# Layer 0's softmax sums and layer 1's transposes by VectorE and transfers, layer 1's moves issued by GpSimd

## The chip, the cores and the metric

The kernel runs on one core of a Trainium2 chip. The metric is the device time of one execution in microseconds (us): a median of 3161.45 us over three runs (3160.39 to 3161.61). A profile records one further execution, engine by engine: PE is TensorE (PEld its weight loads), DVE is VectorE, ACT is ScalarE, POOL is GpSimd, and SPq is the queue in which SyncE issues transfers. PSUM is the memory that TensorE writes; TensorE, VectorE and ScalarE each take their instructions in order.

## What is computed

The input x is (4, 128, 64, 64) in float32: four batches, 128 channels, 4096 tokens each. Two layers follow each other, cut here to what matters:

```python
# layer 0, on _gn(x): q, k, v and gate are 1x1 convolutions with scale and bias
attn = jax.nn.softmax(jnp.einsum('bdn,bdm->bnm', q, k), axis=-1)
out = jnp.einsum('bcm,bnm->bcn', v.reshape(B, -1, N), attn)
x = x + _conv_bn(out.reshape(B, -1, H, W) * gate, Wp, sp, bp)
# layer 1, on tokens t (4, 4096, 128)
q = jnp.einsum('bsd,de->bse', _ln_t(t), W)
t = t + softmax(q @ q.T) @ _ln_t(t)
Wx = batch_norm(_ln_t(t) @ W_ffn.T)        # then a recurrent scan over the tokens
t = t + scan(lambda y, wx: sigmoid(wx + y @ V.T))
```

Both softmaxes need a row sum for each token (the "denominator"), by which the weighted values are divided.

## The kernel before

Each batch is worked through in two stages. The 4096 tokens are cut into 8 blocks of 512 (`NB`, `QB`), and each block into 4 tiles of 128 (`NQ`). Layer 0 (`attention`, lines 178 to 220) takes block n after block n, and for each block 16 pairs of key tiles. Each pair gives two score products (line 200), one exponential on ScalarE (line 202, into one of four buffers `e`), an addition into `acc` on VectorE (lines 207 and 209), and, two pairs later (`LAG`), four weighted products (line 383). Layer 1 (`layer1`, lines 435 to 600) uses that its scores are symmetric: for a pair of blocks (n, a) it computes scores once (line 562), exponentials (line 568), a product with the values (`direct`, line 455), and a second product with the transposed exponentials (`reversed_products`, line 468). The transposed exponentials come from a VectorE transpose of 32x32 squares (line 573) into `dd` and 16 transfers from `dd` to `tt` (line 594), all issued by SyncE. The rows of blocks run in the order 6, 7, 5, 4, 3, 2, 1, 0.

When a block is complete, `finish` appends small closures to the list `pending`; the loops call one of them at each step. Work for the next batch stands in a second list, `ahead`. In layer 0 a block's closures are these:

- `sums`: `denominators` (lines 222 to 233) adds the two halves of `acc` on VectorE (line 224), multiplies each of the 4 tiles by a column of ones on TensorE (line 227, result `md`), and copies and inverts the result (lines 232 and 233). Then `move` turns the residual `xb` into tokens.
- `projection`: one product (line 409) and a `move` of the result into `yt`.
- `tokens`: multiply and add (line 414), layernorm (`layernorm`, lines 250 to 263, whose inverse square root is two GpSimd instructions, lines 116 and 117), and a `move` of the normalised tokens into `ht`.
- `queries`: one product (line 424) on `ht`.

A `move` (lines 235 to 246) transposes 128 x 512 values: a VectorE transpose of 32x32 squares into a buffer `d` (two buffers, line 241), one transfer to a DRAM tile `turn_d` (line 244), and four transfers back (line 246), which wait for the first. All five are issued by SyncE.

In layer 1 a block's closures are `tokens` (row sums at lines 507 and 508, four TensorE transposes of `oacc` into `mt` at line 511, multiply and add at line 513, layernorm), `result` (four TensorE transposes into `mr` at line 523, a ScalarE copy at line 525 and one transfer to `t2_d` at line 526), `turn` (four TensorE transposes of `h2` into `mh` at line 531, a ScalarE copy into `th` at line 532) and `inputs` (one product `mw` on `th` at line 536, statistics and a copy on VectorE at lines 537 and 543, and a transfer at line 544).

The order in which instructions stand on each engine is made at build time by a scheduler from the program and its dependencies; semaphores are put in where one engine needs another's result.

## Time and profile before

| | us |
|---|---|
| median of three runs | 3161.45 |
| the profiled execution | 3160.82 |
| its span, first to last instruction | 3159.1 |
| TensorE busy | 3069.4 |
| VectorE busy | 1797.1 |
| ScalarE busy | 1125.2 |
| GpSimd busy | 140.6 |
| sum products `md`, line 227, 256 records | 33.3 |
| transposes `mt`, line 511, 128 records | 20.0 |
| transposes `mr`, line 523, 128 records | 19.6 |
| transposes `mh`, line 531, 128 records | 28.3 |

Records of one engine overlap, since matmuls are pipelined: what a group occupies is better read from the starts of the instructions around it than from the sum of its records. Each product of 512 columns in float32 shows as two records. Layer 0 of the second batch lies at 820 to 1164 us of the span, its layer 1 at 1164 to 1570; batches three and four follow in the same rhythm, and the recurrent scan is the last 86 us.

### The profile page before, as it was taken

Reading aid. Unit: us, or ns where it says so; the run is one execution under the profiler, and the core shown is the slowest. Engines: PE = TensorE matmul, PEld = TensorE weight load, DVE = VectorE, ACT = ScalarE, POOL = GpSimd, SP = SyncE. Lnnn points to the kernel's source line nnn. Section 1 sums busy time; section 2 is a strip of 40 time slices with the busy share of each in tenths; the row PEclk is TensorE's granted clock in tenths of the full one; section 3 lists DMA queues with packets and bytes.
Section 4 is the critical chain, followed back from the end, with each engine's and each line's share of the span. In section 5 each row is a group of like instructions: output and inputs, shape, how many; then the busy total and the mean of one; then the engine's idle time right before and its main releaser. Section 6 shows DMA issues by size and latency. Waiting matters only on the chain.

```text
span 3159.1 us, 32271 instructions
## 1 busy us (share of the span) xinstructions
PE 3069.4 (97%) x10762; PEld 1374.7 (44%) x10762; DVE 1797.1 (57%) x2970; ACT 1125.2 (36%) x1978; POOL 140.6 (4%) x183
## 2 busy tenths in 40 slices
PE   7999999999999999999999999999999999999976
PEld 3444444444444444444444444444444444444433
DVE  6555556555555555555555555555555555455556
ACT  3433333333333333333333333333333333222324
POOL 0000000000000000000000000000000000000000
PEclk9999999999999999999999999999999999999988
DMA  1111133333111123333211113333321112543333
GB/s 50 34 47 54 54 95 93 91 91 92 51 50 54 54 64 94 94 92 93 74 51 54 54 37 102 92 94 92 91 55 54 54 41 66 146 102 90 99 117 156
DMA packets 233934, 242.17 MB, mean 77 GB/s; under 512 B 88736, under 2 KB 144544, under 8 KB 232736
## 3 DMA queue, kind: packets, MB, share of 16 engines
q1 hardware_dynamic: 233760, 240.02, 27.5%
q8 instruction: 88, 1.44, 0.2%
q14 instruction: 86, 0.70, 0.1%
HBM read 65.80 MB, written 56.62 MB: 39 GB/s over the span
## 4 chain that ended last, share of the span: by engine, by line
PE 89%; DVE 5%; SPq 2%; POOL 1%; DMA 1%; issue 1%; ACT 0%; DVEq 0%; ACTq 0%; POOLq 0%
PE o L383 28%; PE ps L200 15%; PE o L455 13%; PE ps L562 13%; PE ot L468 11%; SPq L594 2%; PE mt L409 1%; PE mw L536 1%; PE mq L424 1%; PE md L227 1%; PE pg L350 1%; PE pqk L315 1%; PE pv L335 1%; PE mh L531 1%; POOL rstd L117 1%
## 5 line engine op out<-in xcount | busy, mean ns | idle before, releaser
L383 PE MATMUL o<-e,nxt 64*128 64x512 f32 x4096 | 965.4, 589 | 0.0
L202 ACT ACTIVATE e<-ps 128x1024 f32<-128x1024 f32 x512 | 521.2, 1024 | 740.6 <-PE ps L200 734.4
L209 DVE TENSOR_TENSOR acc<-acc,e 128x1024 f32<-128x1024 f32 x448 | 546.4, 1220 | 386.7 <-ACT e L202 375.3
L568 ACT ACTIVATE e<-ps,shift 128x512 f32<-128x512 f32 x576 | 391.2, 684 | 772.8 <-PE ps L562 483.2
L383 PEld LDWEIGHTS o<-e,nxt 64*128 64x128 f32 x4096 | 399.5, 187 | 482.7 <-issue 474.6
L562 PE MATMUL ps<-qt 128*128 128x512 f32 x1152 | 546.7, 595 | 3.0 <-ACT e L568 3.0
L200 PE MATMUL ps<-nxt 64*128 64x512 f32 x2048 | 537.9, 603 | 0.3 <-ACT e L202 0.3
L455 PE MATMUL o<-e,h 128*128 128x512 f32 x1152 | 533.4, 592 | 0.0
L468 PE MATMUL ot<-tt,h 128*128 128x512 f32 x896 | 406.6, 597 | 3.6 <-DMA tt<-dd 3.5
L573 DVE STREAM_TRANSPOSE dd<-e 128x512 f32<-128x512 f32 x448 | 288.7, 685 | 109.0 <-ACT e L568 61.3
L455 PEld LDWEIGHTS o<-e,h 128*128 128x128 f32 x1152 | 216.9, 190 | 260.2 <-issue 259.0
L562 PEld LDWEIGHTS ps<-qt 128*128 128x128 f32 x1152 | 211.8, 191 | 243.2 <-issue 222.7
L200 PEld LDWEIGHTS ps<-nxt 64*128 64x128 f32 x2048 | 188.8, 187 | 245.4 <-issue 161.2
L468 PEld LDWEIGHTS ot<-tt,h 128*128 128x128 f32 x896 | 170.2, 191 | 218.2 <-issue 214.1
L473 DVE TENSOR_REDUCE slots<-tt 128x4 f32<-128x2048 f32 x112 | 252.8, 2258 | 8.6 <-DMA tt<-dd 8.2
L482 DVE TENSOR_TENSOR oacc<-oacc,ot 128x512 f32<-128x512 f32 x88 | 59.9, 681 | 209.2 <-PE ot L468 209.2
L116 POOL TENSOR_SCALAR rstd<-mv 128x4 f32<-128x4 f32 x64 | 14.5, 227 | 2518.9 <-DVE mv L257 2518.9
L568 ACT ACTIVATION_READ_ACCUMULATOR e<-ps,shift 128x1 f32 x576 | 113.1, 196 | 0.0
L401 POOL TENSOR_SCALAR xb<-xb,bpc 128x512 f32<-128x512 f32 x32 | 53.6, 1676 | 323.9 <-DMA xb<-in_x_dram 301.5
L117 POOL TENSOR_TENSOR rstd<-rstd,mhalf 128x4 f32<-128x4 f32 x64 | 66.4, 1037 | 5.3
L700 PE MATMUL ps_r<-y,w 128*128 128x256 f32 x168 | 53.0, 440 | 9.7 <-ACT y L697 6.2
L260 DVE TENSOR_SCALAR h<-t,mv,rstd 128x128 f32<-128x128 f32 x128 | 35.7, 343 | 45.2 <-POOL rstd L117 45.2
(113 smaller groups left out, 1411.8 us busy)
## 6 DMA issues: line engine op xcount, KB each, us to landing
tt<-dd SPq DMA_DIRECT2D x1792, 64.0 KB, 2.0
turn_d<-d SPq DMA_DIRECT2D x96, 256.0 KB, 2.0
t_d<-t SPq DMA_DIRECT2D x64, 256.0 KB, 2.0
nxt<-in_x_dram SPq DMA_DIRECT2D x16, 512.0 KB, 6.4
xb<-in_x_dram SPq DMA_DIRECT2D x32, 256.0 KB, 2.9
t<-turn_d SPq DMA_DIRECT2D x128, 64.0 KB, 2.0
yt<-turn_d SPq DMA_DIRECT2D x128, 64.0 KB, 2.0
ht<-turn_d SPq DMA_DIRECT2D x128, 64.0 KB, 2.0
```

The source lines that it names most:

```text
L117: nc.gpsimd.tensor_tensor(dst, dst, mhalf[:, :n], ALU.pow)
L200: nc.tensor.matmul(ps[:, h, :], lhsT=lhsT, rhs=rhs, start=True, stop=True)
L202: nc.scalar.activation(e, ps, AF.Exp, scale=scale)
L209: nc.vector.tensor_tensor(acc, acc, e, ALU.add)
L383: nc.tensor.matmul(o[r], lhsT=v[rs, p + h * PAIRS, :], rhs=e[rs, h, :], start=(p == 0 and h == 0), stop=(p == PAIRS - 1 and h == 1),)
L455: nc.tensor.matmul(o, lhsT=h[:, NQ * a + 2 * i + half, :], rhs=e[:, half, :], start=(a == n and i == 0 and half == 0), stop=(a == 0 and i ...
L468: nc.tensor.matmul(ot, lhsT=h[:, NQ * n + j, :], rhs=t[:, :, j, :, :].rearrange("q p k j -> q k p j"), start=(j == 0), stop=(j == NQ - 1),)
L473: nc.vector.tensor_reduce(slots[:, bass.ts(n, NQ), a], t.rearrange("q p b k j -> q b p (k j)"), AX.XY, ALU.add,)
L562: nc.tensor.matmul(ps[:, half, :], lhsT=qt[:, bass.ts(at, P)], rhs=qt[:, bass.ts(n, QB)], start=True, stop=True,)
L568: nc.scalar.activation(e[:, half, :], ps[:, half, :], AF.Exp, bias=shift, accum_out=slots[:, at, n : n + 1],)
L573: nc.vector.transpose(d.rearrange("q f b k j -> q k b f j")[:, 2 * i + half], e[:, half, :].rearrange("q (b f j) -> q b f j", b=NQ, f=NQ),)
L594: nc.sync.dma_start(t[bass.ts(f, 32), p], d[bass.ts(p, 32), f])
```

## The change

- Layer 0: `denominators` no longer uses TensorE. After the addition of the halves, VectorE transposes 32x32 squares of `acc` into `dq`, reduces 128 x 512 to 128 x 16, and five transfers (one to a DRAM tile `den_d`, four back into `rq`) bring the partial sums to their tokens. A small reduction in `tokens` completes them.
- Layer 1: for all but the last batch's blocks 0 and 1 (`late`), the transposes of `oacc` and of `h2` become `move`s whose transfers are issued by GpSimd (`nc.gpsimd`), `turn` falls away, and the closure `tokens` is cut in two (`weighted`, `tokens`) with empty closures between. For all blocks, `result` becomes a VectorE transpose and four transfers by SyncE, in place of four TensorE transposes, a ScalarE copy and one transfer.
- Work from `ahead` is now also taken along with closures that hold no TensorE work (`light`). The two `acc` buffers become one tile. After the first block of each layer 0, whatever is left in `pending` is called at once (`flush`).

```diff
-                        acc = accp.tile([P, 2, QB], F32, tag="acc", name="acc", bufs=2)
+                        acc = accs[:, n % 2]
...
+                    if n == 0 and p == PAIRS - 1:
+                        flush()
...
-        def denominators(acc, at, rinv):
+        def denominators(acc, at):
             nc.vector.tensor_tensor(acc[:, 0, :], acc[:, 0, :], acc[:, 1, :], ALU.add)
-            m = ps_m.tile([P, NQ], F32, tag="m", name="md")
-            for j in range(NQ):
-                nc.tensor.matmul(
-                    m[:, j : j + 1], lhsT=acc[:, 0, bass.ts(j, P)], rhs=ones,
-                    start=True, stop=True,
-                )
-            den = den_all[:, at : at + NQ]
-            nc.vector.tensor_copy(den, m)
-            nc.vector.reciprocal(rinv, den)
-
-        def move(blocks, dst):
+            d = work.tile([P, 16, 32], F32, tag="d", name="dq", bufs=2)
+            nc.vector.transpose(d, acc[:, 0, :].rearrange("p (b k) -> p b k", k=32))
+            r = stat.tile([P, 16], F32, tag="r", name="r", bufs=2)
+            nc.vector.tensor_reduce(r, d, AX.X, ALU.add)
+            via = den_d[n_moves % len(den_d)]
+            rq = stat.tile([P, 4, NQ], F32, tag="rq", name="rq", bufs=2)
+            nc.sync.dma_start(via, r)
+            for f in range(4):
+                nc.sync.dma_start(
+                    rq[bass.ts(f, 32)],
+                    via[:, bass.ts(f, NQ)].rearrange("(p k) j -> k p j", p=4),
+                )
+            return rq
+
+        def move(blocks, dst, queue=nc.sync):
...
-            nc.sync.dma_start(via, d)
+            queue.dma_start(via, d)
             for a in range(4):
-                nc.sync.dma_start(dst[bass.ts(a, 32)], via[:, a].rearrange("(p i) j k -> i p j k", p=4))
+                queue.dma_start(dst[bass.ts(a, 32)], via[:, a].rearrange("(p i) j k -> i p j k", p=4))
...
                 def tokens():
+                    den = den_all[:, at : at + NQ]
+                    nc.vector.tensor_reduce(den, parts[0].rearrange("q p j -> q j p"), AX.X, ALU.add)
+                    nc.vector.reciprocal(rinv, den)
...
+                late = b == B - 1 and n < 2
+                def weighted():
                     at = (B + b) * NT + n * NQ
                     den = den_all[:, at : at + NQ]
                     nc.vector.tensor_reduce(den, slots[:, bass.ts(n, NQ), :], AX.X, ALU.add)
                     nc.vector.reciprocal(rinv, den)
-                    m = ps_m.tile([P, NQ, P], F32, tag="m", name="mt")
-                    for j in range(NQ):
-                        nc.tensor.transpose(m[:, j, :], oacc[:, n, bass.ts(j, P)], ident)
+                    if not late:
+                        move(oacc[:, n, :].rearrange("c (j f k) -> c j f k", j=NQ, f=4), ot, nc.gpsimd)
+                def tokens():
...
-                    layernorm(quarters(t1), quarters(h2))
+                    layernorm(tiles(t), quarters(h2))
+                    if not late:
+                        move(
+                            h2.rearrange("q j (p i) -> q j p i", p=4),
+                            th.rearrange("c (f j k) -> c f j k", f=4, j=NQ), nc.gpsimd,
+                        )
                 def result():
-                    m = ps_m.tile([P, QB], F32, tag="m", name="mr")
-                    for j in range(NQ):
-                        nc.tensor.transpose(m[:, bass.ts(j, P)], t1[:, j, :], ident)
-                    t2 = work.tile([P, QB], F32, tag="xb", name="t2")
-                    nc.scalar.copy(t2, m)
-                    nc.sync.dma_start(t2_d[b, :, cs], t2)
+                    d = work.tile([P, 4, NQ, 32], F32, tag="d", name="d", bufs=2)
+                    nc.vector.transpose(
+                        d.rearrange("q p j k -> q j p k"), t.rearrange("q p j i -> q j p i")
+                    )
+                    to = t2_d[b, :, cs].rearrange("(p i) (f r) -> f i p r", p=4, f=4)
+                    for f in range(4):
+                        nc.sync.dma_start(
+                            to[f], d[bass.ts(f, 32)].rearrange("i p j k -> i p (j k)")
+                        )
...
-                pending.extend([tokens, result, turn, inputs])
+                if late:
+                    pending.extend([weighted, tokens, turn, inputs, result])
+                else:
+                    light.update([weighted, tokens, result])
+                    pending.extend([weighted, nothing, tokens, result, nothing, inputs])
...
-                        if pending:
-                            pending.popleft()()
-                        elif ahead:
+                        item = pending.popleft() if pending else nothing
+                        item()
+                        if item in light and ahead:
                             ahead.popleft()()
```

More of the change, by code (lines that the diff above doesn't have):

```diff
@@ L66, in conv_attn_hybrid_kernel @@
     t_d = dram.tile([B, NB, P, 4, NQ, 32], F32, name="t_d")
+    den_d = [dram.tile([P, 16], F32, name=f"den{i}_d") for i in range(4)]
     turn_d = [dram.tile([P, 4, NQ, 32], F32, name=f"turn{i}_d") for i in range(8)]
@@ L120, in conv_attn_hybrid_kernel @@
     fast(
-        tc, x, out, t_d, t2_d, wxs_d, turn_d,
+        tc, x, out, t_d, t2_d, wxs_d, turn_d, den_d,
         dict(qk=w[:, DQ : DQ + P], vs=w_vs, g=w_g, ps=w_ps, a=w_a, f=w_f, vt=v_t),
@@ L143, in fast @@
 def fast(
-    tc, x, out, t_d, t2_d, wxs_d, turn_d, wt, col, par, par2, bpc, bc, ident, gavg, ones,
+    tc, x, out, t_d, t2_d, wxs_d, turn_d, den_d, wt, col, par, par2, bpc, bc, ident, gavg, ones,
     shift, inv_sqrt, par_ok,
@@ L171, in fast @@
         done = set()
+        light = {nothing}
         def flush(until=None):
@@ L182, in attention @@
             o = None
+            accs = accp.tile([P, 2, 2, QB], F32, tag="acc", name="acc")
             def pop():
@@ L218, in attention @@
                         pending.popleft()()
+                    if n == 0 and p == PAIRS - 1:
+                        flush()
             while fifo:
                 pop()
-        def denominators(acc, at, rinv):
+        def denominators(acc, at):
+            nonlocal n_moves
             nc.vector.tensor_tensor(acc[:, 0, :], acc[:, 0, :], acc[:, 1, :], ALU.add)
-            m = ps_m.tile([P, NQ], F32, tag="m", name="md")
-            for j in range(NQ):
-                nc.tensor.matmul(
-                    m[:, j : j + 1], lhsT=acc[:, 0, bass.ts(j, P)], rhs=ones,
-                    start=True, stop=True,
-                )
-            den = den_all[:, at : at + NQ]
-            nc.vector.tensor_copy(den, m)
-            nc.vector.reciprocal(rinv, den)
-        def move(blocks, dst):
+            d = work.tile([P, 16, 32], F32, tag="d", name="dq", bufs=2)
[9 more added lines that the diff above has]
+                    via[:, bass.ts(f, NQ)].rearrange("(p k) j -> k p j", p=4),
+                )
+            return rq
+        def move(blocks, dst, queue=nc.sync):
             nonlocal n_moves
@@ L267, in tiles, with by_tile @@
             return [t[:, :, j, :] for j in range(NQ)]
+        def by_tile(t):
+            return t.rearrange("c (f j k) -> c j f k", f=4, j=NQ)
         def quarters(t):
@@ L401, in finish @@
                 nc.gpsimd.tensor_scalar(xb, xb, bpc, None, ALU.add)
+                at = b * NT + n * NQ
+                parts = []
                 def sums():
-                    denominators(acc, b * NT + n * NQ, rinv)
-                    move(xb.rearrange("c (j f k) -> c j f k", j=NQ, f=4), t)
+                    parts.append(denominators(acc, at))
+                    move(by_tile(xb), t)
                 def projection():
@@ L409, in projection @@
                     nc.tensor.matmul(m, lhsT=wt["ps"], rhs=og, start=True, stop=True)
-                    move(m.rearrange("c (j f k) -> c j f k", j=NQ, f=4), yt)
+                    move(by_tile(m), yt)
                 def tokens():
+                    den = den_all[:, at : at + NQ]
+                    nc.vector.tensor_reduce(den, parts[0].rearrange("q p j -> q j p"), AX.X, ALU.add)
+                    nc.vector.reciprocal(rinv, den)
                     for j in range(NQ):
@@ L498, in finish @@
                 t = work.tile([P, 4, NQ, 32], F32, tag="t", name="t1", bufs=2)
+                ot = work.tile([P, 4, NQ, 32], F32, tag="og", name="otk")
                 h2 = work.tile([P, NQ, C], F32, tag="h2", name="h2")
                 th = work.tile([P, QB], F32, tag="th", name="th")
-                t1 = work.tile([P, NQ, C], F32, tag="og", name="t1b")
                 nc.sync.dma_start(t, t_d[b, n])
-                def tokens():
+                late = b == B - 1 and n < 2
+                def weighted():
                     at = (B + b) * NT + n * NQ
@@ L508, in tokens @@
                     nc.vector.reciprocal(rinv, den)
-                    m = ps_m.tile([P, NQ, P], F32, tag="m", name="mt")
-                    for j in range(NQ):
-                        nc.tensor.transpose(m[:, j, :], oacc[:, n, bass.ts(j, P)], ident)
+                    if not late:
+                        move(oacc[:, n, :].rearrange("c (j f k) -> c j f k", j=NQ, f=4), ot, nc.gpsimd)
+                def tokens():
+                    src = ot
+                    if late:
+                        m = ps_m.tile([P, NQ, P], F32, tag="m", name="mt")
+                        for j in range(NQ):
+                            nc.tensor.transpose(m[:, j, :], oacc[:, n, bass.ts(j, P)], ident)
+                        src = m.rearrange("q j (p i) -> q p j i", p=4)
@@ L512, in tokens @@
                     for j in range(NQ):
                         nc.vector.scalar_tensor_tensor(
-                            t1[:, j, :].rearrange("q (p i) -> q p i", p=4),
-                            m[:, j, :].rearrange("q (p i) -> q p i", p=4), rinv[:, j : j + 1],
-                            t[:, :, j, :], ALU.mult, ALU.add,
-                        )
-                    layernorm(quarters(t1), quarters(h2))
-                def result():
-                    m = ps_m.tile([P, QB], F32, tag="m", name="mr")
-                    for j in range(NQ):
-                        nc.tensor.transpose(m[:, bass.ts(j, P)], t1[:, j, :], ident)
-                    t2 = work.tile([P, QB], F32, tag="xb", name="t2")
-                    nc.scalar.copy(t2, m)
-                    nc.sync.dma_start(t2_d[b, :, cs], t2)
+                            t[:, :, j, :], src[:, :, j, :], rinv[:, j : j + 1], t[:, :, j, :],
@@ new lines, in tokens @@
+                            ALU.mult, ALU.add,
+                        )
+                    layernorm(tiles(t), quarters(h2))
[4 more added lines that the diff above has]
+                        )
+                def result():
+                    d = work.tile([P, 4, NQ, 32], F32, tag="d", name="d", bufs=2)
[7 more added lines that the diff above has]
+                        )
@@ L530, in turn @@
                     for j in range(NQ):
-                        nc.tensor.transpose(m[:, bass.ts(j, P)], h2[:, j, :], ident)
+                        nc.tensor.transpose(by_tile(m)[:, j], h2[:, j, :], ident)
                     nc.scalar.copy(th, m)
@@ L544, in inputs @@
                         nc.sync.dma_start(wxs_d[b, :, :, bass.ts(n, GB), :], wx)
-                pending.extend([tokens, result, turn, inputs])
+                if late:
+                    pending.extend([weighted, tokens, turn, inputs, result])
+                else:
+                    light.update([weighted, tokens, result])
+                    pending.extend([weighted, nothing, tokens, result, nothing, inputs])
             for n in [NB - 2, NB - 1] + list(range(NB - 3, -1, -1)):
```

## The prediction

> **What bounds the kernel now.** I read the busy shares first, then the busy time by stage (the second batch's layer 0 and layer 1), then the chain of waits.

> ```profile
> PE 3069.4 (97%) x10762; PEld 1374.7 (44%) x10762; DVE 1797.1 (57%) x2970; ACT 1125.2 (36%) x1978; POOL 140.6 (4%) x183
> ```

> ```profile
> 820.00:1164.00 344.00, 344.00 (x1562) 152.06 (x1562) 199.37 (x304) 133.19 (x138) 23.63 (x24) 1.00 0.16 49
> 1164.00:1570.00 406.00, 401.00 (x1066) 181.18 (x1064) 230.75 (x402) 134.88 (x332) 10.93 (x18) 1.00 0.37 94
> ```

> The columns of the stages are stage, length, busy PE, PEld, DVE, ACT, POOL, granted clock, transfer share, GB/s. TensorE has no gap in layer 0 and 5 us in layer 1, at a granted clock of 1.00. So each microsecond taken from TensorE inside the stages is won, and each microsecond for which the next TensorE instruction waits is lost: there is nothing to absorb it. VectorE has 145 us free in this layer 0 and 175 in this layer 1.

> What the removed work occupies I read from TensorE's timeline, by the starts around it:

> ```profile
> 140.69 3.60 PE L383 MATMUL o<-e,nxt 64*128 64x512 f32 x16
> 144.22 1.05 PE L227 MATMUL md<-ones,acc 128*128 128x1 f32 x8
> 145.20 1.99 PE L200 MATMUL ps<-nxt 64*128 64x512 f32 x8
> ```

> ```profile
> 644.67 1.88 PE L562 MATMUL ps<-qt 128*128 128x512 f32 x4
> 646.38 0.65 PE L511 MATMUL mt<-ident,oacc 128*128 128x128 f32 x4
> 646.87 1.45 PE L562 MATMUL ps<-qt 128*128 128x512 f32 x3
> ```

> Sixteen `o` records take 3.43 us in the chain of waits, so the next product could have started at 140.69 + 3.43 = 144.12; it starts at 145.20. One block's sum products cost 1.08 us. A group of four transposes costs 646.87 - 646.38 = 0.49 us.

> **What the change removes.** Sums: 32 blocks x 1.08 = 34.6 us. Transposes: 3 groups x 32 blocks = 96, less the 4 groups (`mt`, `mh`) that the two late blocks keep: 92 x 0.49 = 45.1 us. TensorE's waits in front of them:

> ```profile
> PE mh L531 <- DVE h L260: 14.8, 22, 2.4
> PE mh L531 <- ACT e L568: 2.8, 3, 0.9
> ```

> That is 17.6 us, of which the two late blocks keep 1.1 + 2.4 (the timeline at 3054 and 3063 us), and 1.3 for `mr`: 15.4 us. In all 95.1 us go. ScalarE loses 62 copies of 0.59 us, which is worth nothing by itself: it is 36% busy.

> **What the change puts in their place.** In 30 blocks of layer 1 the product `mw` now waits for a move issued by GpSimd. What a move costs on SyncE is seen in layer 0:

> ```profile
> 150.75 0.34 SPq L244 DMA_DIRECT2D turn_d<-d  x1
> 152.77 1.74 SPq L246 DMA_DIRECT2D yt<-turn_d  x4
> ```

> ```profile
> 150.00 0.72 DVE L241 STREAM_TRANSPOSE d<-mt 128x512 f32<-128x512 f32 x1
> 156.16 1.14 DVE L414 SCALAR_TENSOR_TENSOR t<-yt,rinv,t 128x128 f32<-128x128 f32 x4 [0.23 <-DMA yt<-turn_d]
> ```

> From the end of the transpose (150.72) to the reader (156.16) are 5.44 us: five issues of c = 0.43 us (1.74/4), and 3.3 us in which the first and the last transfer land. I write a move as 5c + 3.3. No transfer issued by GpSimd is in this trace, so c is unknown. Its lower bound is SyncE's 0.43. GpSimd's own instructions are the nearest rows for its side:

> ```profile
> L401 POOL TENSOR_SCALAR xb<-xb,bpc 128x512 f32<-128x512 f32 x32 | 53.6, 1676 | 323.9 <-DMA xb<-in_x_dram 301.5
> L117 POOL TENSOR_TENSOR rstd<-rstd,mhalf 128x4 f32<-128x4 f32 x64 | 66.4, 1037 | 5.3
> ```

> The upper bound is 1.68, a pass over 128 x 512. A transfer here is 128 short runs, so its issue is nearer to the small instruction: I take c = 1.04, hence a move of 8.5 us (5.45 and 11.7 at the ends).

> *The middle of layer 1.* In the built order of the changed kernel I add up TensorE's work, at the durations above (0.857 us per full product of 512 columns, 0.43 per half-height one), between the transpose of `h2` and `mw`. For the first six blocks of batches 0 to 2 it is 9.4, 8.6, 7.7, 8.6, 6.9 and 7.3 us, for the first five of the last batch 8.6, 8.6, 7.7, 8.6 and 6.8. From each go 0.7 us for the transpose itself and 0.67 us by which VectorE's result is late against TensorE's order today (14.8 us in 22 waits). What is left, 5.4 to 8.0 us, hides a move at SyncE's price, and not one of 8.5: the stalls are 0.5, 1.3, 2.2, 1.3, 3.0 and 2.6 = 10.9 us a batch, 32.7 in three, and 9.3 in the last: 42 us. At c = 0.43 it is 0, at 1.68 about 115. The other move, of `oacc`, has 12 to 34 us in these blocks and is hidden. Behind a waiting `mw` stand the next scores and `direct`, so ScalarE and VectorE run dry too and nothing is caught up.

> *The ends of batches 0 to 2.* Blocks 1 and 0 complete in the next layer 0, and the `flush` at its first block's last pair calls the rest without spacing. Four moves then stand in a row on GpSimd: `oacc` and `h2` of block 1, `oacc` and `h2` of block 0. From the last `ot` to the second `mw` the order has 24.0 us of TensorE work. The chain: addition 0.9, transpose 0.7, move 5c + 3.3, tokens and layernorm 4.9 (811.75 to 816.6 us), one `acc` addition 1.2, transpose 0.7, the first transfer of the next move c + 1.7 and its four reads 4c, then block 0's move 5c + 3.3, tokens 4.9, transpose 0.7, move 5c + 3.3. Sum 25.6 + 20c: a stall of 1.6 + 20c, at 1.04 us 22.4, three times 67 us (31 at 0.43, 106 at 1.68). VectorE waits here as well, with the `acc` additions behind it; that lies inside the same chain.

> *The end of the last batch.* Block 2's `mw` (not late) stands 4.3 us of TensorE work behind its last `ot`, and the chain is 0.9 + 4.9 + 0.7 for another addition + 0.7 + 5c + 3.3: a stall of 6.2 + 5c = 11.4 us (8.4 to 14.6).

> *What I cost at nothing.* Layer 0's new VectorE work is a transpose of 0.7 and a reduction of about 0.7 a block, 45 us in 32 blocks, in the 145 us that are free per stage; the wait for the sums' transfers takes the place of VectorE's present wait for `md` (98.4 us in 29 waits, about the same 3.4 us each). If the four `e` buffers didn't cover it, it would cost up to the 45 us. Five more transfers a block on SyncE lie in a queue that is mostly idle in layer 0. Layer 1's third VectorE transpose (0.7) is within its 175 free us. `result` issues three more transfers a block on SyncE, 30 x 3 x 0.63 = 57 us on a queue that is nearly full in the first rows (133 issues in 94.6 us); they are due only at the end, but `tt` stands behind them, with four steps of slack. At worst 57 us.

> [...] The row above (133 issues without a gap) shows that issue time is what SyncE lacks, so I take the row: the sum would be no better with SyncE as issuer. [...]

> **The sum.** The profiled execution's time is 3160.8 (span 3159.1 and 1.7 around it). 3160.8 - 95.1 + 42 + 67 + 11.4 = 3186 us. The median shown is 0.6 us higher, which I leave out. At c = 0.43: 3160.8 - 95.1 + 0 + 31 + 8.4 = 3105. At c = 1.68: 3160.8 - 95.1 + 115 + 106 + 14.6 = 3301. From the lower end to my value the time rises 81 us for 0.61 of c, 133 per us; it crosses today's at c = 0.85.

> **Rivals.**
> - *GpSimd issues nearly as fast as SyncE* (not slower; decides below c = 0.85). Then the middle stalls almost vanish and the ends of the batches remain. At c = 0.6: 3105 + 0.17 x 133 = 3128 us. For it: an issue needs no arithmetic on the data, and every 64 KB transfer between SBUF and DRAM in this trace lands a median of 2.0 us after its issue. Against it: even GpSimd's 128 x 4 instruction takes 1.04 us.
> - *The gain and the stalls cancel* (c from 0.80 to 0.90): 3161 us, within 6 us.
> - *Layer 0 gives its part back as well* (slower still): VectorE stands at the small reduction until `rq` has landed and runs more than the four `e` buffers behind, so TensorE waits in each block. It decides if VectorE's wait per block goes above about 6 us (two pairs of 2.8) from today's 3.4. All of 34.6 us lost: 3186 + 35 = 3221 us. Against it: VectorE is 58% busy and has caught up by the next pair or two.

> **How the numbers follow.** This kernel's runs tell 0.2% (6 us) from no change. Chances: the forecast's stalls decide, 0.47; they and layer 0 too, 0.07; cancel, 0.05; GpSimd fast, 0.41. So slower 0.54, same 0.05, faster 0.41. The forecast's own range is 3167 to 3233 (c from 0.9 to 1.3); the range given reaches to 3106 for the fast rival, and to 3245, where layer 0 or a GpSimd issue of 1.37 us would stand.

> **What would show it.** Right: TensorE busy about 80 us lower, `mw` led by waits on the transfers into `th` of 1 to 3 us in mid-layer and about 10 at the ends of batches, and GpSimd's issues near 1 us apart. Wrong: waits of `mw` under 15 us in all, or issues under 0.7 us; or TensorE's new waits in front of `ps` and `ot` instead (`e` late, `tt` late), which would mean VectorE or SyncE is the new bound.

## The result, and the profile after

| | before | after |
|---|---|---|
| median, us (4 runs each, same chip) | 3161.53 | 3297.44 |
| lowest to highest, us | 3160.39 to 3161.82 | 3290.82 to 3305.02 |
| profiled execution, its span, us | 3160.82, 3159.1 | 3299.83, 3298.0 |
| TensorE idle in the span, us | 89.7 | 241.1 |
| mean granted clock of TensorE | 0.992 | 0.966 |

The change made the kernel slower: the ratio is 1.0431, 95% interval 1.0414 to 1.0449. The forecast was slower, but with 3186 us, and its range ended at 3245.

The busy shares of the kernel after:

```profile
PE 3057.0 (93%) x10138; PEld 1330.7 (40%) x10138; DVE 1892.2 (57%) x3126; ACT 1089.0 (33%) x1916; POOL 305.2 (9%) x483
```

TensorE has 624 instructions fewer, and its busy time fell by 12 us only. The busy time by stage, for the second batch's layer 0 and layer 1 (columns as before: stage, length, PE, PEld, DVE, ACT, POOL, granted clock, transfer share, GB/s):

```profile
811.00:1219.00 408.00, 378.26 (x1595) 161.56 (x1594) 236.61 (x379) 138.34 (x142) 37.59 (x52) 0.95 0.17 51
1219.00:1599.00 380.00, 367.08 (x892) 163.24 (x890) 221.34 (x371) 122.28 (x314) 40.71 (x70) 0.99 0.43 113
```

Layer 0, which had no gap before, now has 30 us of gaps and a clock of 0.95. From the first score product of each stage to that of the next, its four stages lasted 383, 368, 368 and 368 us before and 403, 408, 409 and 411 after. TensorE's waits (engine, line, waited for: us in total, times, longest):

```profile
PE mw L576 <- DMA th<-turn_d: 83.9, 28, 10.2
PE mt L430 <- DVE og L412: 66.0, 28, 3.6
```

The first was forecast, at 120 us. The second, in layer 0, was not. VectorE's own waits name what stands ahead of `og`:

```profile
DVE den_all L435 <- DMA rq<-den_d: 155.6, 32, 6.4
```

VectorE's timeline at the end of one block of layer 0 (start, length, instruction, and in brackets the idle time before it and what ended it):

```profile
185.92 0.69 DVE L234 TENSOR_TENSOR acc<-acc 128x512 f32<-128x512 f32 x1
186.65 0.71 DVE L236 STREAM_TRANSPOSE dq<-acc 128x512 f32<-128x512 f32 x1
187.28 0.67 DVE L255 STREAM_TRANSPOSE d<-xb 128x512 f32<-128x512 f32 x1
187.88 0.64 DVE L238 TENSOR_REDUCE r<-dq 128x16 f32<-128x512 f32 x1
193.98 0.18 DVE L435 TENSOR_REDUCE den_all<-rq 128x4 f32<-128x16 f32 x1 [5.46 <-DMA rq<-den_d]
...
194.28 0.66 DVE L411 TENSOR_TENSOR og<-o,og 128x512 f32<-128x512 f32 x1
194.98 0.69 DVE L412 TENSOR_TENSOR og<-og,nxt 128x512 f32<-128x512 f32 x1
```

The small reduction is written in `tokens`, two closures behind `projection`, but in the built order it stands ahead of the two `og` operations on which `projection`'s product `mt` waits. `og`, which needs no transfer, starts at 194.28, behind the reduction and the reciprocal; the reduction waited 5.46 us for `rq`. TensorE's timeline there:

```profile
191.12 1.88 PE L401 MATMUL o<-e,nxt 64*128 64x512 f32 x8
195.73 1.71 PE L430 MATMUL mt<-og,w 128*128 128x512 f32 x2 [2.73 <-DVE og L412]
197.37 2.08 PE L205 MATMUL ps<-nxt 64*128 64x512 f32 x4
```

`mt` starts 2.73 us late, and then takes 1.71 us where the same product took 1.13 before. The busy time and the granted clock (0.50) of three neighbouring stretches show why (columns as above):

```profile
192.70:196.10 3.40, 0.67 (x3) 0.30 (x2) 2.05 (x5) 0.00 (x0) 1.30 (x1) 1.00 0.24 59
196.10:199.51 3.41, 3.41 (x8) 1.12 (x8) 2.56 (x3) 0.02 (x1) 0.00 (x0) 0.50 0.02 5
199.51:202.92 3.41, 3.41 (x18) 1.49 (x18) 1.23 (x1) 1.74 (x2) 0.00 (x0) 0.99 0.35 121
```

In the stretch with the stall TensorE was busy for 0.67 of 3.40 us. In the next its clock is half, and it finishes 8 instructions where the one after finishes 18.

A ledger can be made from this. As "slow clock" it counts half of the time in which TensorE was busy at 0.50; "work" is its busy time less that. This split is an estimate; e3 and e12, which take the same work from TensorE, bear it out with -34.7 and -35.6 us at 49.0 and 2.4 us of slow clock. The three differences against the kernel before (work 3060.7, idle 89.7, slow clock 8.7 us) add up to the difference of the spans, within rounding. Each row is one execution. "After" is the changed kernel; e1 to e13 are the experiments below.

| profiled execution | span | work | idle | slow clock | sum |
|---|---|---|---|---|---|
| after | 3298.0 | -85.9 | +151.4 | +73.4 | +138.9 |
| e1, sums behind `mt` | 3190.3 | -84.4 | +87.9 | +27.7 | +31.2 |
| e2, layer 1's part alone | 3228.9 | -49.0 | +88.6 | +30.2 | +69.8 |
| e3, layer 0's part alone | 3248.6 | -34.7 | +75.2 | +49.0 | +89.5 |
| e4, stalls filled | 3259.4 | -24.6 | +100.4 | +24.4 | +100.2 |
| e5, batch ends by TensorE | 3203.1 | -73.2 | +73.1 | +44.1 | +44.0 |
| e6, `h2` by TensorE | 3147.0 | -62.4 | +29.5 | +20.8 | -12.1 |
| e7, both moves by SyncE | 3181.3 | -89.0 | +73.2 | +38.1 | +22.3 |
| e8, e5 and e7 together | 3192.9 | -73.1 | +59.8 | +47.1 | +33.8 |
| e9, e6 with preparation spaced | 3130.8 | -63.2 | +17.6 | +17.3 | -28.3 |
| e10, e6 with `result` by TensorE | 3157.7 | -52.4 | +32.7 | +18.3 | -1.4 |
| e11, e6 with its move by SyncE | 3140.2 | -69.3 | +34.8 | +15.7 | -18.8 |
| e12, layer 0's part, behind `mt` | 3133.6 | -35.6 | +7.6 | +2.4 | -25.6 |
| e13, e9 with its move by SyncE | 3129.4 | -67.6 | +28.3 | +9.7 | -29.6 |

### The profile page after: what moved, and what is told of

The parts are those of the page before. It is cut to its first block, busy times and chain, and to the rows that moved or that the text cites. A ratio compares the mean times of both kernels' runs of the same rounds, so it can differ in the third digit from the quotient of the medians.

```text
span 3298.0 us, 32108 instructions
## 1 busy us (share of the span) xinstructions
PE 3057.0 (93%) x10138; PEld 1330.7 (40%) x10138; DVE 1892.2 (57%) x3126; ACT 1089.0 (33%) x1916; POOL 305.2 (9%) x483
## 5 line engine op out<-in xcount | busy, mean ns | idle before, releaser
L401 PE MATMUL o<-e,nxt 64*128 64x512 f32 x4096 | 980.9, 597 | 0.0
L401 PEld LDWEIGHTS o<-e,nxt 64*128 64x128 f32 x4096 | 408.6, 192 | 509.1 <-issue 501.5
L205 PE MATMUL ps<-nxt 64*128 64x512 f32 x2048 | 560.0, 626 | 0.3 <-ACT e L207 0.3
L606 PE MATMUL ps<-qt 128*128 128x512 f32 x1152 | 537.9, 597 | 0.0
L205 PEld LDWEIGHTS ps<-nxt 64*128 64x128 f32 x2048 | 197.6, 194 | 280.2 <-issue 196.0
L576 PE MATMUL mw<-th,w 128*128 128x512 f32 x64 | 47.1, 826 | 85.7 <-DMA th<-turn_d 83.9
L274 DVE TENSOR_SCALAR h<-t,mv,rstd 128x128 f32<-128x128 f32 x256 | 71.4, 343 | 92.2 <-POOL rstd L118 92.2
L117 POOL TENSOR_SCALAR rstd<-mv 128x4 f32<-128x4 f32 x64 | 14.5, 227 | 1049.6 <-DVE mv L271 1049.6
L430 PE MATMUL mt<-og,w 128*128 128x512 f32 x64 | 44.4, 782 | 66.0 <-DVE og L412 66.0
```

Source lines behind the costliest of these rows:

```text
L205: nc.tensor.matmul(ps[:, h, :], lhsT=lhsT, rhs=rhs, start=True, stop=True)
L274: nc.vector.tensor_scalar(dst[j], src[j], mv[:, j, 0:1], rstd[:, j : j + 1], ALU.subtract, ALU.mult,)
L401: nc.tensor.matmul(o[r], lhsT=v[rs, p + h * PAIRS, :], rhs=e[rs, h, :], start=(p == 0 and h == 0), stop=(p == PAIRS - 1 and h == 1),)
L606: nc.tensor.matmul(ps[:, half, :], lhsT=qt[:, bass.ts(at, P)], rhs=qt[:, bass.ts(n, QB)], start=True, stop=True,)
```

## The experiments

**One order on VectorE (e1).** The reduction and the reciprocal get an ordering edge behind the transpose of `mt`; nothing else changes (`move` now returns its VectorE transpose, `parts[1]`).

```diff
-                    move(by_tile(m), yt)
+                    parts.append(move(by_tile(m), yt))
...
-                    nc.vector.tensor_reduce(den, parts[0].rearrange("q p j -> q j p"), AX.X, ALU.add)
-                    nc.vector.reciprocal(rinv, den)
+                    with tc.issue_after(parts[1].ins):
+                        nc.vector.tensor_reduce(den, parts[0].rearrange("q p j -> q j p"), AX.X, ALU.add)
+                        nc.vector.reciprocal(rinv, den)
```

> The changed kernel with one order on VectorE altered: the small reduction of the sums and the reciprocal are issued behind the transpose of `mt`, not ahead of the `og` operations. Same instructions, same transfers. Theory A (layer 0 loses because VectorE, which works in order, stands at the small reduction until `rq` has landed, and `og` and with it `mt` stand behind; each stall of TensorE also costs about half of a 3.4 us stretch at half clock): the 66 us of waits of `mt` go, and 28 x 1.7 = 48 us of slow clock with them: 3297 - 114 = 3183 us. Rival B (layer 0 loses because of the added VectorE work, 1.4 us a block, and the added transfers themselves): the same work is done, only the place of the wait moves: 3285 to 3300 us. Rival C (only the waits count, the clock recovers by itself): 3297 - 66 = 3231 us.

Measured: 3195.54 us (ratio to before 1.0112, 1.0095 to 1.0128), 102 us below the changed kernel. VectorE's timeline at the same place:

```profile
187.31 0.69 DVE L412 TENSOR_TENSOR og<-o,og 128x512 f32<-128x512 f32 x1 [1.71 <-ACT og L411]
188.03 0.69 DVE L413 TENSOR_TENSOR og<-og,nxt 128x512 f32<-128x512 f32 x1
...
191.41 0.70 DVE L255 STREAM_TRANSPOSE d<-mt 128x512 f32<-128x512 f32 x1
192.04 0.13 DVE L437 TENSOR_REDUCE den_all<-rq 128x4 f32<-128x16 f32 x1
```

`rq` has landed by the time the reduction comes up, and no `mt` wait is left among TensorE's. The ledger splits the gain: 63 us less idle time, 46 us less slow clock. Theory A holds, 12 us above its 3183; about 5 of these are waits of `mq` for `ht` (6.5 us, against 1.7 in the changed kernel). B is out, and C too, which left the clock out.

**Each part alone (e2, e3).** e2 is the changed kernel with the sums by products against ones as before (and the addition of the halves written in the changed token order). e3 is the kernel before with the changed `denominators` and the small reduction in `tokens` (the partial sums written in the old token order).

```diff
 e2
-                    parts.append(denominators(acc, at))
+                    denominators(acc, at, rinv)
 e3
-                    denominators(acc, b * NT + n * NQ, rinv)
+                    parts.append(denominators(acc, at))
```

> The changed kernel with layer 0's sums done by TensorE products against ones as before (the sum of the two halves is written in the changed token order into another tile, so that the weights stay contiguous); layer 1 as changed. Theory A (both parts lose, each by its own waits): layer 1's part gains 45 + 15 and loses 86 us of waits for `mw` and about 15 stretches of slow clock of 1.7 to 3 us, some 30 us: 3161 - 60 + 86 + 30 = 3217 us. Rival D (layer 1's part gains by itself and only layer 0's stalls spoil it, since the two share VectorE and SyncE's queue): 3161 - 60 + 40 = 3141 us or less. By the prediction's own terms for layer 1 (45.1 + 15.4 gained, 120 lost) 3221 us.

> The kernel before with layer 0's part alone: sums by VectorE's transpose and reduction and the transfers through DRAM; layer 1 as before. Theory A: 3161 - 35 + 66 (28 waits of `mt` of 2.36 us) + 28 x 1.7 (slow clock) = 3240 us, with VectorE's waits at the small reduction near 5 us each. The prediction on record costed this part at nothing beyond its gain: 3161 - 35 = 3126 us. Its rival (layer 0 gives its 35 us back): 3161 us.

Measured: e2 3232.20 us (1.0221, 1.0203 to 1.0239), e3 3249.53 us (1.0276, 1.0259 to 1.0293). Each part loses alone, 71 and 88 us; together 159, where the whole change lost 136. In the ledger the two rows together have 12 us more idle time, 6 more slow clock and 2 more work than the whole change. In e3 TensorE's waits are led by the same line:

```profile
PE mt L429 <- DVE og L411: 72.0, 28, 3.4
```

So layer 1's part is not needed for it, and rival D is out.

**The stall filled (e4).** Two more products go into `mt` ahead of the real one, weights by weights, and are overwritten.

```diff
+                    for _ in range(2):
+                        nc.tensor.matmul(m, lhsT=wt["ps"], rhs=w4, start=True, stop=True)
                     nc.tensor.matmul(m, lhsT=wt["ps"], rhs=og, start=True, stop=True)
```

> The changed kernel with two more products of 512 columns into `mt` ahead of the real one (weights against weights, overwritten by it), which wait for nothing but the bank: TensorE is occupied for 1.7 of each 2.36 us in which it stood, and `mt` itself becomes ready no earlier. Theory A (a stall of more than about 2 us makes the granted clock drop to half for 3.4 us, which costs 1.7 us): the drops in layer 0 go: 3297 - 28 x 1.7 + 7 (four first blocks, which have no stall to fill) = 3256 us, with TensorE's mean granted clock back near 0.98. Rival (the drops have another cause, such as the load of VectorE or the transfers): clock as in the changed kernel, 0.966, and 3297 to 3305 us.

Measured: 3256.77 us (1.0300, 1.0283 to 1.0317): 41 us faster by adding work. TensorE's timeline at such a place:

```profile
236.95 1.98 PE L432 MATMUL mt<-w 128*128 128x512 f32 x4
239.76 1.13 PE L433 MATMUL mt<-og,w 128*128 128x512 f32 x2 [0.83 <-DVE og L413]
240.81 1.13 PE L206 MATMUL ps<-nxt 64*128 64x512 f32 x4
```

`mt` still waits for the same `og`, but after it each product takes its usual time. The stretches at half clock fall from 42 to 14. By the ledger the added products cost 61 us of work and take away 51 us of idle time; the gain is the 49 us of slow clock. What e4 takes away is idle time, and 28 of the 42 stretches at half clock go with it.

**Where layer 1's part loses (e5, e6, e7, e8).** All four start from e1.

```diff
 e5
-                late = b == B - 1 and n < 2
+                late = n < 2
 e6: the move of h2 goes, turn comes back
-                    pending.extend([weighted, nothing, tokens, result, nothing, inputs])
+                    pending.extend([weighted, nothing, tokens, result, turn, inputs])
 e7 (e8 has e5's and e7's edits)
-                        move(oacc[:, n, :].rearrange("c (j f k) -> c j f k", j=NQ, f=4), ot, nc.gpsimd)
+                        move(oacc[:, n, :].rearrange("c (j f k) -> c j f k", j=NQ, f=4), ot, nc.sync)
...
-                            th.rearrange("c (f j k) -> c f j k", f=4, j=NQ), nc.gpsimd,
+                            th.rearrange("c (f j k) -> c f j k", f=4, j=NQ), nc.sync,
```

> The kernel with the sums' reduction behind `mt` (3195.5 us), and blocks 1 and 0 of every batch, not of the last alone, with their transposes on TensorE instead of the two moves on GpSimd. Theory (the two `mw` waits at each batch's end, 5.3 and 7.6 us, and the 20 to 24 us at half clock there are the price of four moves in a row): 3 x 13 = 39 us of waits go and about 25 of the slow clock's 32, against 6 us of transposes and about 7 us of waits for `h2` a batch, as in the last batch: 3195.5 - 39 - 25 + 6 + 21 = 3158 us. Rival (the chain of VectorE's work in these two blocks is as long without the moves, the flush calls it without spacing either way): the waits move from `mw` to `mh`, 3190 us or more.

> The kernel with the sums' reduction behind `mt` (3195.5 us), and `h2` transposed by TensorE in all blocks, as before the change; `oacc` still goes by the move and `t2` by VectorE. Theory (every wait of `mw` comes from the second move; the first is hidden by 12 us and more of TensorE work except at batch ends): 86 us of `mw` waits and most of 44 us of slow clock go, 30 x 0.49 = 15 us of transposes and 17 us of `mh` waits come back, and at batch ends some 5 us a block stay for the first move, with their clock 45 us in all: 3195.5 - 86 - 44 + 15 + 17 + 45 = 3142 us. Rival (the first move is not hidden either): `mh` waits of over 3 us in mid-layer, 3190 us.

> The kernel with the sums' reduction behind `mt` (3195.5 us), and layer 1's moves issued by SyncE instead of GpSimd. Theory (what a GpSimd move costs above SyncE's 5.4 us, about 1.7 us, is what makes the mid-layer waits of 1.2 us, and SyncE's queue has room): mid-layer waits go (24 x 1.2 = 28), the ends lose about 6 us a batch (18) and some 10 us of slow clock: 3140 us. Rival (the reason for a second issuer: in layer 1 SyncE issues without a gap, so that the move stands behind 16 transfers into `tt`, and later `tt` behind the move): `mw` waits stay or grow and `ot` waits appear for `tt`, 3195 us or more.

> The two edits before together: batch ends by TensorE, the other moves issued by SyncE. If both theories hold and add up: 3158 - 28 - 5 = 3125 us, below both kernels. If SyncE's queue is the limit: 3158 us or more, with `mw` waits of 1 us and more in mid-layer.

Measured: e5 3201.55 us (1.0122, 1.0100 to 1.0144), no better than e1. Its waits:

```profile
PE mw L578 <- DMA th<-turn_d: 46.8, 22, 9.6
PE mh L573 <- DVE h L275: 23.6, 8, 4.9
```

The two `mw` waits at a batch's end (5.3 and 7.6 us) became `mh` waits of 2.9 and 2.6 us, for VectorE's chain. By the ledger that is 15 us less idle time (18 were expected), but 11 us more work and 16 us more slow clock, where 25 less were expected. The shorter waits took nothing off the slow clock: at the batch ends it costs 24.5 us, against 21.0 in e1. The other 13 us of it lie elsewhere, where the waits are much the same; no run explains them, and the four runs of e5 spread over 15 us.

e6 3151.49 us (0.9972, 0.9962 to 0.9981), faster than the kernel before. The `mw` waits are gone, and what came in their place is short:

```profile
PE mh L568 <- DVE h L275: 26.7, 25, 4.9
```

So the second move, of `h2`, was the larger part of layer 1's loss, 44 us; the first is hidden in mid-layer, as forecast, where the `mh` waits are 0.7 to 0.8 us each, against 0.4 to 0.7 in the kernel before.

e7 3183.67 us (1.0074, 1.0057 to 1.0091), 12 us faster than with GpSimd:

```profile
PE mw L578 <- DMA th<-turn_d: 33.8, 8, 8.6
PE ot L494 <- DMA tt<-dd: 20.8, 8, 9.2
```

Both sides were partly right: the mid-layer `mw` waits vanish, and `ot` now waits for `tt`, all 8 times in the last batch. e8 3189.51 us (1.0090, 1.0073 to 1.0107): the two edits don't add up. Against e7 it has 13 us less idle time, but 16 more work and 9 more slow clock, 8 of them at the batch ends; the mid-layer waits of `mw` that the rival named are not there.

**What is worth keeping (e9 to e13).** e9, e10 and e11 start from e6; e12 is e3 with e1's edge; e13 is e9 with e11's edit.

```diff
 e9
-                    light.update([weighted, tokens, result])
 e10: result as before the change (t1 takes a buffer of d)
+                        nc.tensor.transpose(by_tile(m)[:, j], t1[:, j, :], ident)
 e11
-                        move(oacc[:, n, :].rearrange("c (j f k) -> c j f k", j=NQ, f=4), ot, nc.gpsimd)
+                        move(oacc[:, n, :].rearrange("c (j f k) -> c j f k", j=NQ, f=4), ot, nc.sync)
```

> The kernel before with layer 0's part alone, and in it the small reduction ordered behind the transpose of `mt`. Theory (the part's gain is the TensorE work it removes, 34.6 us, and its whole loss is VectorE's place of waiting): 3161 - 35 = 3126 us, no waits of `mt`, half-speed stretches as before. Rival (VectorE's added 45 us or the sums' transfers cost something of their own): 3140 us or more.

Measured: 3132.90 us (0.9907, 0.9892 to 0.9922), 29 us below the kernel before. The second batch's layer 0 has no gap and a clock of 1.00 again:

```profile
806.00:1166.00 360.00, 360.00 (x1585) 156.32 (x1582) 223.16 (x345) 143.73 (x163) 26.98 (x26) 1.00 0.18 54
```

Its stages last 359.7 us three times, against 368.0 before: 8.3 us for 8 blocks of 1.08 us (8.6) of sum products. The 7 us above the expected 3126 are matched by waits of `mq` for `ht`: 8.8 us in 4 waits, 4.9 of them in the last batch, against 0.6 before.

> The kernel with the reduction behind `mt` and `h2` transposed by TensorE (3151.5 us), and also `t1` transposed by TensorE and stored by one transfer, as before the change. The prediction cost the 90 added transfers and the added VectorE transposes of `t2` at nothing: then the 30 groups of transposes come back with 15 us and the waits for `mr` with 1 to 3 us: 3168 us. Rival (the transfers on SyncE and the third VectorE transpose do cost, up to 57 us): 3151 us or less.

Measured: 3157.87 us (0.9988, 0.9979 to 0.9997). `result` by VectorE and transfers is worth 6 us, not 16. By the ledger work rose by 10 us and idle time by 3, and slow clock fell by 3. The waits of `mh` fell from 26.7 to 14.7 us, which the expectation left out. In their place `mr` waits 6 us and `mt` 10 us in 3 waits: at the batch ends VectorE stands 6.1 to 7.4 us at the transpose of `xb`, for GpSimd, and `og` again stands behind it.

> The kernel with the reduction behind `mt` and `h2` transposed by TensorE (3151.5 us), with the remaining move of `oacc` issued by SyncE. The move is hidden from either queue: if SyncE's queue has room, 3151 us; if the five more transfers a block make `tt` late, as the 21 us of `ot` waits with both moves on SyncE suggest, some 10 us of `ot` waits with their slow clock: 3160 to 3170 us.

Measured: 3141.98 us (0.9936, 0.9922 to 0.9949), 9.5 us faster than by GpSimd: against both expectations, and `ot` waits 5.4 us, against 4.5 in e6. By the ledger there is 7 us less work and 5 less slow clock against 5 more idle time; why, no run shows.

> The kernel with the reduction behind `mt` and `h2` transposed by TensorE (3151.5 us), where the next batch's preparation goes beside the empty items only, no longer beside `weighted`, `tokens` and `result`. Theory (the waits of `pv` for VectorE, 15 us with 2.6 us each beside a stretch of slow clock, come from preparation put beside VectorE's heavy items): 3151.5 - 15 - 6 = 3131 us. Rival (what is put off is called in a row at the layer's end and waits there): 3151 us or more.

Measured: 3132.54 us (0.9907, 0.9892 to 0.9922), the number that the theory gave. Its mechanism holds in part: the named waits of `pv` fell from 15.4 to 10.3 us, not to nothing, of 12 us less idle time in all.

> The kernel with the reduction behind `mt`, `h2` transposed by TensorE and preparation beside empty items only (3132.5 us), with the move of `oacc` issued by SyncE. Layer 0's part alone, in the right order, took 3132.9 us, so so far layer 1's part is worth nothing beside it. If the queue of GpSimd is what eats its 31 us (the same change of queue gained 9.5 us at 3151.5), the two edits add up: 3123 us. If the two gains were one and the same (fewer waits of `pv` in both), 3132 us.

Measured: 3135.98 us (0.9923, 0.9910 to 0.9937), not to be told from e9: the gains of e9 and e11 don't add up. So e9, with layer 0's part and what is left of layer 1's, equals e12, with layer 0's alone, although e9 has 27.6 us less TensorE work by the ledger. It gives them back as 10 us of idle time and 15 us of slow clock. Two of e9's waits are longer; e12 has 14.3 us of the first (longest 2.0) and 2.7 us, one wait, of the second:

```profile
PE mh L568 <- DVE h L275: 23.7, 25, 4.9
PE pv L354 <- DVE nxt L346: 10.3, 4, 2.7
```

Each of the four `pv` waits of 2.6 us is followed by a stretch at half clock (at 26, 487, 1231 and 1975 us); e12 has only the first of these. The other added stretches lie at the batch ends and in the last batch. Which of VectorE's new items makes these waits was not tried.

## Why the prediction was right or wrong

- **Removed work: right.** 79.7 us of TensorE work were forecast (34.6 + 45.1); the ledger has 85.9. Layer 0's part alone has 34.7 and 35.6 in e3 and e12.
- **The step that failed: layer 0 "costed at nothing".** The prediction put it thus: "the wait for the sums' transfers takes the place of VectorE's present wait for `md`". It compared the two waits' lengths and looked for the cover in the `e` buffers. It didn't ask what stands behind the wait on VectorE: `og`, and behind that `mt`. The kernel before shows that this chain has little room:

```profile
140.65 0.69 DVE L224 TENSOR_TENSOR acc<-acc 128x512 f32<-128x512 f32 x1
145.31 0.16 DVE L232 COPY den_all<-md 128x4 f32<-128x4 f32 x1 [3.97 <-PE md L227]
...
146.30 0.69 DVE L394 TENSOR_TENSOR og<-og,nxt 128x512 f32<-128x512 f32 x1
```

```profile
148.84 1.13 PE L409 MATMUL mt<-og,w 128*128 128x512 f32 x2
```

  From the last addition to the end of `og` took 6.34 us there (146.99 - 140.65), and `mt` came at 8.19: 1.85 us of room. After the change it takes 9.75 us (195.67 - 185.92), while TensorE, without the sum products, is there 1.08 us sooner, at 7.1. 9.75 - 7.1 = 2.65, and the wait shown is 2.73. All but the 5.46 us of the transfers could have been added up beforehand, and for these the prediction had the price of a move, 5.44. Measured: 66 us of stalls, and with the clock 88 us lost in e3 instead of 35 won.
- **Not in the sum at all: the clock.** Every stall was priced at its own length. 73 us of the 139 are the slow clock after stalls. The 28 stalls of layer 0 are 2.36 us each (66.0/28), and by their own length alone e4, which adds 61 us of work for 51 us less idle time, would have lost 10 us: it won 41, with 49 us less slow clock, 1.75 us for each stall.
- **GpSimd's issue: mis-sized, in the safe direction.** c was taken as 1.04 us from a row of arithmetic; it is 0.55 (2.20/4) in GpSimd's timeline, under the 0.7 us that the prediction itself named as a sign of being wrong:

```profile
856.91 0.63 POOL L258 DMA_DIRECT2D turn_d<-d  x1 [2.19 <-DVE d L255]
859.88 2.20 POOL L260 DMA_DIRECT2D th<-turn_d  x4 [2.33 <-DMA turn_d<-d]
```

```profile
863.75 2.05 PE L576 MATMUL mw<-th,w 128*128 128x512 f32 x2 [5.24 <-DMA th<-turn_d]
```

  The move took 6.8 us from the issue to `mw` (863.75 - 856.91), against 5.44 on SyncE and 8.5 forecast; the transfers landed later than SyncE's (medians of 2.9 against 2.0 us to DRAM, 2.4 against 1.9 back). The waits of `mw` were 36 us in mid-layer (42 forecast), 38 at the ends of batches 0 to 2 (67), 10.2 in the last batch (11.4). The formula for the ends, 1.6 + 20c, gives 12.6 us at c = 0.55; 12.3 to 13.0 were measured, though the move shown took 0.8 us more than its 5c + 3.3 = 6.05, so that other terms of that chain must be too high.
- **SyncE as issuer: a row misread.** The prediction took the row of 133 issues without a gap to show that SyncE lacks issue time, and so that SyncE as issuer would be no better. That row joins issues across pauses: they take 79.8 of the 94.6 us, with pauses of 3.6 and 4.6 us among them, and over the first batch's layer 1 SyncE issues for 74% of the time. It waits there for VectorE (us in total, times, longest, in the kernel before):

```profile
SPq L594 <- DVE dd L573: 125.2, 44, 7.2
```

  So issue time was not what SyncE lacked, and with SyncE as issuer the kernel was 12 us (e7) and 9.5 us (e11) faster.
- **The rivals.** "GpSimd fast" had its condition met (c below 0.85) and still lost 71 us in e2, 30 of them slow clock. "Layer 0 gives its part back" named VectorE's wait at the small reduction, but put its price at 35 us and its threshold at 6 us through the `e` buffers; it struck at 4.9 us (155.6/32) through `og`, for 123 us.
- **The sign was right by luck, and the size wrong.** For layer 1 alone the mechanism holds: 84 us of `mw` waits against 60.5 won (45.1 + 15.4), and e2 is slower. But the sum also counted layer 0's 34.6 us as won: with the waits as measured it gives 3160.8 - 95.1 + 84 = 3150 us, and by the prediction's own line at c = 0.55 3105 + 0.12 x 133 = 3121, both faster than before. What made the kernel slower is what the sum left out. From the forecast to the profiled execution: 3186 + 66 (stalls of `mt`) + 73 (clock) - 36 (`mw` waits forecast too high) - 6 (more work gone) = 3283; the rest to 3299.8 is `pv` (9 us more), `mh` (about 3.5 more than was counted) and small waits.

## What to carry to other kernels

When a wait moves to another source, list what is queued behind it on that engine, and add up that chain to the first instruction of the bounding engine that needs it, with its room today: comparing the lengths of the two waits says nothing. Where a small consumer of a transfer may be issued early, tie it behind the work that doesn't need the transfer; one ordering edge was worth 102 us here. Where TensorE is the bounding engine, look at the granted clock beside the length of its stalls: here 28 stalls of 2.36 us went with 49 us of slow clock, about 1.7 us each, so they were worth filling, as in e4 (41 us), before work is taken off TensorE. Shortening the waits at the batch ends from 5.3 and 7.6 to 2.9 and 2.6 us, as in e5, took nothing off the slow clock there.
